# A graph transformer layer and a graph attention layer on one core: the raw weight blocks renumbered so that each load is one contiguous run, and new lists for the first and the last steps

## The chip, the core and the metric

The kernel runs on one core of a Trainium2 chip. The metric is the device time of one launch in microseconds (us). PE is TensorE, DVE is VectorE, ACT is ScalarE, POOL is GpSimd, SP is the engine that only issues transfers here.

## What is computed

There are 128 graphs of 128 nodes with 512 features, in fp32. The first layer is attention with 8 heads on a normalised input, with scores scaled by twice the adjacency; the second is graph attention with one softmax.

```python
h = jnp.maximum(_layernorm(x, axis=-1), 0.0)
q, k, v = (proj(Wq, bq), proj(Wk, bk), proj(Wv, bv))
scores = jnp.einsum('bhqd,bhkd->bhqk', q, k) * SCALE
scores = scores * (adj + adj)[:, None]
x = x + softmax(scores) @ v @ Wo.T + bo
h = jnp.maximum(_layernorm(x, axis=-1), 0.0)
Wh = h @ W
e = leaky_relu(Wh @ a[:512] + swapaxes(Wh @ a[512:], 1, 2))
x = x + elu(softmax(where(adj > 0.5, e, -9e15), axis=1) @ Wh)
```

## The kernel before, in words

**Tiling.** Two graphs make a pair (64 pairs, N = 64), two pairs make a group of four graphs. All work for a pair or group is cut into named steps, and three lists written out by hand say in which order the steps are issued. Each engine, and the transfer queue on SP, takes its own steps strictly in that order.

**Fewer products.** Q, K and V of a group are not the plain 4 x 4 x 4 block product. A fast multiplication scheme gets by with 26 block products for each of Q, K and V (TERMS), at the price of sums of blocks of the tokens (FORMS, on POOL) and of the weights (WSUMS, on DVE, made once). The weight blocks live in `w_sb`, 28 slots of three 128 x 128 blocks (Q, K and V). The sixteen raw blocks of the weights are loaded into slots 0 to 15 and many are then overwritten in place by sums.

```python
def load_blocks(n):
    nc.sync.dma_start(w_sb[:, n : C * C : C], wT[:, n : C * C : C])
def block_sum(k):
    d, a, op, b = WSUMS[k]
```

C is 4, so load n fetches slots n, n+4, n+8 and n+12: on each partition four runs of 1536 bytes. The host writes `wT` in the order of the slots.

**The lists.** HEAD (730 steps, `step@pair`) starts the kernel; ORDER (341 steps, `step:lag`) is repeated for 27 groups; TAIL (1051 steps, `step@pair`, counted back from 64) ends it. A step that has been issued is not issued again.

```python
for step, p in HEAD: do(step, p)
for g in range(EARLY, N // 2 - LATE):
    for step, lag in ORDER: do(step, 2 * g - lag)
for step, p in TAIL: do(step, N + p)
```

**Names of steps.** Several act for a later pair than the one written: with `@p`, `l0` and `t0`, `t1`, `s0` serve pair p+5, `f0`, `lT`, `hd0`, `hd1` pair p+4, and `T`, `Q`, `V`, `A`, `B` the next group.

- `lx` (L96, L98) loads a pair of x, `l0` (L103) loads x early for the statistics, `t0` and `t1` (L204 to L207, DVE) are the row statistics, `pp` (L212, POOL) the inverse root.
- `hn` (L229, DVE), `tp` (L236, PE), `ev` (L239, ACT): normalise, transpose and keep the hidden tokens `hA` of the first four pairs. Later pairs load x transposed (`lT`, L115), spread the statistics through memory (`s0`, L247; `f0`, L252) and normalise in place (`hd0` on POOL, L262; `hd1` on DVE, L264).
- `L0` to `L3` (L160) load the weight blocks, `W0` to `W34` (L166 and L169, DVE) form their sums.
- `T` (L281, POOL) forms a token sum `tf`. `Q` (L296) and `V` (L305) are the products on PE, `A` (L320 on ACT for a first take, L322 on DVE after it) and `B` (L333, L335) take them out of PSUM.
- `sc` (L373, PE), `at`, `mx`, `ex`, `rc`, `nm`: scores and softmax of a graph, `a` or `b` of the pair. `fl` (L408, DVE) turns 32 x 32 blocks, `bl` (L412, SP) sends them to memory, `pl` (L418, SP, four transfers) brings them back transposed as `aT`, `pc` (L441, PE) is the context product.
- `o0` to `o6` (L348, PE) and `od` (L455, DVE): the seven products of the output projection and their sums. `st`, `pw`, `nm`, `h2`, `d`, `px`, `pd`, `pv`, `wm`, `pr`, `m1`, `e1`, `sw`: second norm and second softmax. `g` (L534, PE), `ge` (L540, ACT), `w0` to `w6` (L348, PE), `zc` (L548, ACT), `wd` (L552, DVE): second layer.
- `lt` (L123, SP) loads the transposed adjacency. `fa` and `fb` (L564, L568, DVE) finish a pair, `so` (L574, SP) stores it; the last pair is finished in quarters (`qe`, `qa`, `qb`) and stored by `qs1`, `qs2`, `qs0` (L571, SP).

**What sets the order.** PE waits only where a step's input is not there or where none of eight PSUM banks is free. An engine that waits holds everything behind it in its own list, and SP does so too: a store that waits for its data holds the loads listed after it.

Of the kernel before, what the change touches and what calls it, by code (L numbers as in the profile page):

```python
# [13 lines left out]
P = 128  # L14
# [10 lines left out]
def kernel(  # L25
# [16 lines left out]
    nc = tc.nc  # L42
    B, S, E = x.shape
    C = E // P
# [22 lines left out]
    def sums(text):  # L67
# [7 lines left out]
        1,8,7,13- 0,10,18,10- 1,9,19,03- 0,11,0,00- 1,1,20,01+ 0,2,16,. 1,13,5,11+ 0,0,21,03- 1,12,6,12- 0,0,1,02-  # L75
        1,14,14,02- 0,18,24,00+ 0,3,26,01+ 3,20,15,03+ 2,21,22,02- 3,19,25,13+ 2,22,23,12- 3,16,9,11- 2,6,10,.
        3,17,27,01- 2,4,2,13+ 3,15,4,00- 2,4,3,10- 3,23,12,10- 2,24,8,12+ 2,7,13,11-
# [5 lines left out]
        7=15-7 16=8-4 17=15-11 18=17-16 0=1-0 19=7-18 19=19-0 9=9n11 11=9n15 5=5-11 20=5-7 6=6n5 5=14n6 21=15-3  # L83
        21=21-0 22=10n17 23=1n2 24=23-22 25=24-15 3=3+1 1=25+3 14=14n22 24=12n24 26=13-12 27=11-12 2=7+2 2=3+2 4=11-4
        3=3n19 17=8-17 12=17-12 8=19+20 8=5-8 11=5+11 13=11-13
# [55 lines left out]
    w_sb = const.tile([P, SLOTS, 3, P], F32, name="w3")  # L141
# [16 lines left out]
    def load_blocks(n):  # L158

        nc.sync.dma_start(w_sb[:, n : C * C : C], wT[:, n : C * C : C])  # L160
# [55 lines left out]
    st0, rows0, qks, vs, scs, ats, trs, blocks, aTs, pcs = ({} for _ in range(10))  # L216
# [408 lines left out]
    def listed(text, mark):  # L625
# [3 lines left out]
        lx@1 t0@-4 t1@-4 lx@0 t0@-5 pp@1 hn1@1 tp1@1 ev1@1 hn0@1 L0@0 L3@0 W2@0 W0@0 t1@-5 pp@0 W1@0 lx@2 t1@-3 tp0@1  # L629
        ev0@1 T0@-2 hn1@0 tp1@0 ev1@0 T4@-2 T8@-2 L1@0 W7@0 hn0@0 W4@0 W3@0 V0@-2 B0@-2 tp0@0 ev0@0 W8@0 W5@0 W13@0  # L630
        W9@0 Q0@-2 A0@-2 W6@0 T1@-2 Q2@-2 T2@-2 V1@-2 l0@-2 t0@-2 L2@0 t1@-2 V2@-2 T3@-2 B1@-2 V3@-2 B3@-2 B2@-2
        W14@0 Lu@0 W10@0 pp@3 hn0@3 Q1@-2 A1@-2 la@-1 W16@0 W11@0 V5@-2 V7@-2 B7@-2 Q3@-2 A2@-2 Q4@-2 V4@-2 A3@-2
        W15@0 hn1@3 W17@0 W19@0 W12@0 W18@0 W21@0 B4@-2 W20@0 W29@0 W31@0 Q5@-2 Q7@-2 A7@-2 W22@0 Lo1@0 W24@0 A4@-2
        T5@-2 Q6@-2 V6@-2 tp1@3 A6@-2 Q8@-2 Q9@-2 B6@-2 V8@-2 A8@-2 W25@0 V9@-2 Lc@0 l0@0 t1@0 T7@-2 t0@-3 t0@0 T9@-2
        T10@-2 A9@-2 Q11@-2 A11@-2 ev1@3 B9@-2 W23@0 V11@-2 tp0@3 T6@-2 Q10@-2 B8@-2 ev0@3 W26@0 W28@0 T11@-2 T12@-2
        Q13@-2 s0@0 A13@-2 A10@-2 V10@-2 Q12@-2 W27@0 W33@0 Q15@-2 A15@-2 A12@-2 B10@-2 T13@-2 V14@-2 Q14@-2 V13@-2
        B13@-2 B11@-2 A14@-2 Q17@-2 A17@-2 B14@-2 pp@2 V15@-2 V12@-2 B15@-2 T16@-2 T14@-2 Q16@-2 A16@-2 hn1@2 V16@-2
        B16@-2 Q19@-2 A19@-2 Q18@-2 Q20@-2 l0@-1 t1@-1 Q21@-2 V18@-2 V17@-2 A20@-2 hn0@2 A21@-2 W30@0 B17@-2 Q22@-2
        A22@-2 B12@-2 W32@0 T0@0 t0@-1 Q0@0 T15@-2 V20@-2 Q23@-2 A23@-2 sca@0 Lo0@0 Wo0@0 Lw0@0 scb@0 ata1@0 ata0@0
        Q24@-2 A0@0 tp0@2 ev0@2 V0@0 B20@-2 V22@-2 mxa@0 exa3@0 exa2@0 W34@0 tp1@2 l0@2 la@0 B22@-2 V24@-2 V19@-2  # L640
        ev1@2 A24@-2 Q25@-2 Lw1@0 B0@0 B24@-2 atb1@0 t1@2 t0@2 atb0@0 V25@-2 B19@-2 rca1@0 lT@0 exa1@0 exa0@0 rca0@0
        s0@-1 T1@0 T2@0 T4@0 V2@0 B2@0 Q2@0 A2@0 nma1@0 Q1@0 V1@0 Q4@0 B1@0 V21@-2 T3@0 V3@0 Wo1@0 A1@0 Q3@0 V4@0
        B25@-2 A4@0 B3@0 nma3@0 cu00@0 V5@0 A25@-2 B21@-2 mxb@0 l0@1 t0@1 t1@1 A3@0 s0@2 B4@0 nma2@0 nma0@0 fla@0
        V7@0 V23@-2 T5@0 Q6@0 A6@0 Q5@0 Q7@0 B7@0 exb1@0 A7@0 sca@1 V6@0 exb3@0 Q8@0 cu01@0 f0@0 hd0@0 V9@0 ata1@1
        exb2@0 ata0@1 rcb1@0 B6@0 V8@0 exb0@0 rcb0@0 Ww0@0 Q9@0 mxa@1 A8@0 B9@0 B8@0 lT@1 bla@0 T6@0 Q10@0 V10@0
        hd1@0 f0@1 scb@1 s0@1 nmb2@0 nmb1@0 nmb3@0 nmb0@0 flb@0 blb@0 pla@0 T7@0 T8@0 T9@0 T10@0 T11@0 T12@0 exa0@1
        atb0@1 atb1@1 V11@0 B11@0 ccp@0 V13@0 Q13@0 Wo3@0 Wo2@0 B10@0 exa3@1 A9@0 A10@0 mxb@1 A13@0 sup0@0 exb3@1
        Q11@0 A11@0 l0@4 B13@0 exa1@1 T13@0 Q14@0 V12@0 B12@0 A14@0 rca0@1 V15@0 exa2@1 B15@0 Q12@0 V14@0 plb@0
        exb0@1 Q15@0 V17@0 A12@0 Ww1@0 B14@0 exb2@1 exb1@1 rca1@1 rcb1@1 nmb3@1 nmb2@1 sua0@0 T14@0 Q16@0 hd0@1 B17@0
        V19@0 A15@0 rcb0@1 Q17@0 hd1@1 T0@2 nma2@1 nma0@1 Ww3@0 ccd@0 A16@0 t1@4 B19@0 V16@0 B16@0 A17@0 pca@0 pea@0  # L650
        nmb0@1 pcb@0 T7@2 nma1@1 o0@0 o1@0 sh@0 V21@0 B21@0 nma3@1 V18@0 Q18@0 Q20@0 sh@2 od0@0 peb@0 nmb1@1 cs0@0
        sh@1 cs2@0 cs1@0 o2@0 fla@1 bla@1 od1@0 V20@0 Q19@0 o3@0 od2@0 o4@0 flb@1 A19@0 Q21@0 A20@0 Q22@0 B23@-2
# [12 lines left out]
        T14@2 mxb@3 exb3@3 exa3@3 exb1@3 Q17@2 A17@2 T13@2 exb2@3 V14@2 B14@2 w0@0 w1@0 zc0@0 d00@1 cs0@2 d10@1
        rca0@3 o0@2 od0@2 V16@2 exb0@3 exa2@3 Q14@2 gs1@0 A14@2 cs2@2 px@1 d11@1 nma0@3 B16@2 Q19@2 o1@2 rcb0@3
        nmb1@3 w2@0 zc2@0 Q16@2 V18@2 V20@2 cs1@2 gs3@0 o2@2 w4@0 A16@2 rca1@3 cs3@2 B20@2 Ww2@0 nma1@3 l0@6 w3@0
        nma3@3 nma2@3 od2@2 rcb1@3 A19@2 fla@3 V22@2 B22@2 pd@1 pv@1 bla@3 Q18@2 Q20@2 o3@2 zc4@0 w5@0 wd4c@0 nmb3@3
        nmb0@3 nmb2@3 flb@3 od1@2 T0@4 A20@2 wm@1 Q21@2 A21@2 zc5@0 V17@2 wd1@0
# [23 lines left out]
        w6@-10 blb@-7 plb@-7 pla@-7 o4@-8 od4@-8 T16@-8 B17@-8 wd6@-10 od4c@-8 Q22@-8 A22@-8 o5@-8 pr@-9 ez@-10 m1@-9  # L693
        e1@-9 fa@-10 o6@-8 od6@-8 Q24@-8 V24@-8 V19@-8 Q0@-6 A0@-6 sw@-9 g0@-9 g1@-9 ge1@-9 ge0@-9 B19@-8 od5@-8
        B24@-8 V21@-8 T15@-8 s0@-7 f0@-6 fb@-10 st0@-8 so@-10 Q23@-8 V25@-8 A24@-8 Q25@-8 A23@-8 gs0@-9 B25@-8 st1@-8
        sca@-6 ata1@-6 ata0@-6 scb@-6 pcb@-7 peb@-7 atb0@-6 pw@-8 nm@-8 h20@-8 pca@-7 atb1@-6 h21@-8 T1@-6 Q2@-6
        w0@-9 w1@-9 B21@-8 V23@-8 pea@-7 o0@-7 mxa@-6 exa3@-6 zc0@-9 gs1@-9 gs2@-9 d00@-8 exa2@-6 exa1@-6 B23@-8
        mxb@-6 gs3@-9 A25@-8 T2@-6 V1@-6 T4@-6 T5@-6 o1@-7 w2@-9 exa0@-6 T3@-6 B1@-6 V3@-6 lT@-6 Q1@-6 lx@-7 sh@-7
        od0@-7 exb2@-6 cs0@-7 cs2@-7 od1@-7 zc2@-9 cs1@-7 rca1@-6 exb1@-6 exb0@-6 w4@-9 o2@-7 lT@-5 T8@-6 d10@-8
        rca0@-6 nma1@-6 px@-8 pd@-8 zc4@-9 A1@-6 w3@-9 pv@-8 od2@-7 cs3@-7 rcb0@-6 wd1@-9 hd0@-6 o4@-7 od4@-7 wd4c@-9  # L700
        hd1@-6 d11@-8 exb3@-6 A2@-6 V0@-6 nma0@-6 nmb0@-6 Q3@-6 o3@-7 nmb1@-6 B3@-6 d01@-8 rcb1@-6 B0@-6 o5@-7 od5@-7
        od4c@-7 w6@-9 wd6@-9 st0@-7 Q4@-6 o6@-7 V2@-6 nma2@-6 A3@-6 B2@-6 od6@-7 w5@-9 st1@-7 pw@-7 T7@-6 T9@-6
        nma3@-6 wm@-8 fla@-6 bla@-6 nm@-7 V5@-6 V7@-6 T10@-6 nmb3@-6 pr@-8 m1@-8 f0@-5 B7@-6 V4@-6 Q5@-6 Q7@-6 sca@-5
        nmb2@-6 flb@-6 blb@-6 B4@-6 A4@-6 Q6@-6 V9@-6 A7@-6 lt@-6 zc5@-9 fa@-9 Q9@-6 e1@-8 sw@-8 A6@-6 Q8@-6 ez@-9
# [235 lines left out]
```

## Time and profile before

| | us |
|---|---|
| Median of 3 runs | 2327.14 (2325.97 to 2329.51) |
| The profiled execution, its own time | 2323.18 |
| Its span, first to last instruction | 2321.4 |
| Outside the span | 1.8 |
| PE busy in the span | 2291.4 |
| DVE busy | 2099.9 |
| ACT busy | 1460.3 |
| POOL busy | 972.8 |

In this execution the steps of HEAD run until PE is at about 168.8 us, the 27 rounds of ORDER until 2084.5 us (70.95 us a round), and TAIL to the end. A busy share is an average: the head, the rounds and the tail have their own limits, so the views are read by stretches of time. The busy time of PE is a sum of modelled, overlapping ends; the distance between the starts of two matmuls tells more.

### The profile page before, as it was taken

What the parts mean: (1) busy time and instruction counts of PE and PEld (TensorE: products, weight loads), DVE (VectorE), ACT (ScalarE), POOL (GpSimd) and SP (SyncE); (2) the same over time, 40 slices, a digit from 0 to 9 for tenths busy, and PEclk for the clock granted to TensorE, in tenths of its full rate; (3) what the DMA queues carried; (4) which work ended last, traced back from release to release, by engine and by line L of the source; (5) the groups of instructions that cost most, each with busy time, mean ns of one, the idle gap of its engine ahead of it and who ended that gap; (6) DMA issues with size and microseconds to landing.
All of it is one profiled execution on the core that took longest, in us unless ns stands there. A gap on an engine that the chain in (4) does not pass through costs nothing.

```text
span 2321.4 us, 45352 instructions
## 1 busy us (share of the span) xinstructions
PE 2291.4 (99%) x15444; PEld 2037.5 (88%) x15444; DVE 2099.9 (90%) x4620; ACT 1460.3 (63%) x4942; POOL 972.8 (42%) x1112
## 2 busy tenths in 40 slices
PE   8999999999999999999999999999999999999998
PEld 6888888888888888888888888888888888888986
DVE  8998999998999999999989999999999899999897
ACT  2566666666665766666666657666666666566665
POOL 3634443443443444434434434444344344344211
PEclk9999999999999999999999999999999999999999
DMA  4544654545544545545455455454454554544432
GB/s 164 148 119 119 157 137 135 148 120 145 151 124 138 144 121 157 135 137 148 120 145 150 124 139 139 125 157 134 137 143 126 145 150 124 139 125 124 119 121 89
DMA packets 267471, 314.60 MB, mean 136 GB/s; under 512 B 23656, under 2 KB 193640, under 8 KB 267240
## 3 DMA queue, kind: packets, MB, share of 16 engines
q1 hardware_dynamic: 263736, 311.57, 48.6%
q8 instruction: 123, 2.02, 0.4%
q0 software_dynamic: 1920, 0.13, 0.1%
q14 instruction: 108, 0.88, 0.1%
q10 hardware_dynamic: 1584, 0.01, 0.0%
HBM read 210.77 MB, written 100.85 MB: 134 GB/s over the span
## 4 chain that ended last, share of the span: by engine, by line
PE 92%; DVE 4%; DMA 1%; ACT 1%; issue 1%; POOL 1%; SPq 0%; POOLq 0%; DVEq 0%; ACTq 0%
PE acc_q L296 30%; PE row_a L348 24%; PE acc_v L305 14%; PE row_c L348 9%; PE pc L441 5%; PE sc L373 5%; PE pg L534 5%; DVE st L204 1%; DVE w L169 1%; DVE qk L322 1%; ACT z L548 1%; DMA aT<-blocks 0%; DMA w<-in_wT 0%; DVE junk L478 0%; DVE x L455 0%
## 5 line engine op out<-in xcount | busy, mean ns | idle before, releaser
L296 PE MATMUL acc_q<-tf,w 128*128 128x256 f32 x2176 | 550.1, 384 | 2.2 <-DVE w L169 1.6
L281 POOL TENSOR_TENSOR tf<-hA,tf 128x256 f32<-128x256 f32 x288 | 225.0, 786 | 660.7 <-PE acc_v L305 642.4
L296 PEld LDWEIGHTS acc_q<-tf,w 128*128 128x128 f32 x2176 | 393.0, 190 | 63.0 <-ACT qk L320 8.4
L392 ACT ACTIVATE at<-at,nmx 128x128 f32<-128x128 f32 x1024 | 397.5, 391 | 35.8 <-DVE nmx L387 33.7
L322 DVE TENSOR_TENSOR qk<-qk,acc_q 128x512 f32<-128x512 f32 x512 | 341.8, 678 | 31.6 <-PE acc_q L296 28.4
L305 PEld LDWEIGHTS acc_v<-w,tf 128*128 128x128 f32 x2176 | 312.4, 191 | 24.7 <-POOL tf L281 2.1
L348 PE MATMUL row_a<-w,gT 128*128 128x256 f32 x1272 | 327.7, 384 | 4.3 <-ACT gT L540 0.7
L401 ACT ACTIVATE at<-at,rs 128x128 f32<-128x128 f32 x1024 | 329.1, 396 | 1.2 <-DVE rs L396 1.2
L305 PE MATMUL acc_v<-w,tf 128*128 128x128 f32 x2176 | 321.6, 275 | 1.9 <-POOL tf L281 1.8
L348 PE MATMUL row_a<-wo,cxT 128*128 128x256 f32 x1272 | 320.9, 382 | 0.8 <-DVE x L455 0.5
L296 PE MATMUL acc_q<-hA,w 128*128 128x256 f32 x1152 | 295.3, 380 | 0.0
L348 PEld LDWEIGHTS row_a<-w,gT 128*128 128x128 f32 x1272 | 233.6, 190 | 42.3 <-ACT z L548 8.5
L348 PEld LDWEIGHTS row_a<-wo,cxT 128*128 128x128 f32 x1272 | 231.5, 190 | 37.3 <-DVE x L455 10.0
L335 DVE TENSOR_TENSOR v<-v,acc_v 128x256 f32<-128x256 f32 x512 | 206.2, 408 | 33.1 <-PE acc_v L305 31.7
L296 PEld LDWEIGHTS acc_q<-hA,w 128*128 128x128 f32 x1152 | 208.7, 190 | 27.3 <-DVE qk L322 4.3
L380 DVE SCALAR_TENSOR_TENSOR at<-sc,adj 128x512 f32<-128x512 f32 x256 | 166.1, 681 | 44.3 <-PE sc L373 44.2
L478 DVE SCALAR_TENSOR_TENSOR junk<-h,u 128x512 f32<-128x512 f32 x256 | 200.2, 782 | 3.4 <-ACT h L471 1.0
L281 POOL TENSOR_TENSOR tf<-hA 128x256 f32<-128x256 f32 x128 | 93.4, 741 | 257.8 <-PE acc_v L305 194.0
L548 ACT COPY z<-row_a 128x256 f32<-128x256 f32 x256 | 93.3, 364 | 163.3 <-PE row_a L348 158.6
L392 ACT ACTIVATION_READ_ACCUMULATOR at<-at,nmx 128x1 f32 x1024 | 194.0, 189 | 0.0
L320 ACT ACTIVATE qk<-acc_q,bq 128x256 f32<-128x256 f32 x256 | 120.1, 469 | 113.7 <-PE acc_q L296 113.6
L269 POOL TENSOR_TENSOR x<-x,c 128x512 f32<-128x512 f32 x128 | 174.9, 1386 | 22.5 <-DMA x<-in_x 9.5
(97 smaller groups left out, 4162.8 us busy)
## 6 DMA issues: line engine op xcount, KB each, us to landing
blocks<-tr SPq DMA_DIRECT2D x128, 512.0 KB, 5.5
aT<-blocks SPq DMA_DIRECT2D x512, 128.0 KB, 3.5
x<-in_x SPq DMA_DIRECT2D x123, 512.0 KB, 4.0
out<-x SPq DMA_DIRECT2D x63, 512.0 KB, 3.3
hA<-in_xT SPq DMA_DIRECT2D x120, 256.0 KB, 4.1
mr<-rows SPq DMA_DIRECT2D x60, 256.0 KB, 3.2
adj<-in_adj SPq DMA_DIRECT2D x64, 128.0 KB, 2.2
adjT<-in_adjT SPq DMA_DIRECT2D x64, 128.0 KB, 5.5
```

The lines of the kernel that those rows point to most:

```text
L269: nc.gpsimd.tensor_tensor(xs[p][:, i, :], xs[p][:, i, :], c_sb, OP.add)
L281: eng.tensor_tensor(forms[g, 2 * C + k], form(g, a), form(g, b), OP.add if op == "+" else OP.subtract)
L296: nc.tensor.matmul(acc[:, i, :], w_sb[:, slot, i, :], form(g, f), start=fresh and i == 0, stop=True, skip_group_check=True)
L305: nc.tensor.matmul(acc[:, i, :], form(g, f)[:, i * P : (i + 1) * P], w_sb[:, slot, 2, :], start=fresh and i == 0, stop=True, skip_group_ch ...
L320: nc.scalar.activation(d[:, i, :], acc[:, i, :], AF.Identity, bias=bias[:, j : j + 1], scale=float(sign))
L322: nc.vector.tensor_tensor(d, d, acc, OP.add if sign > 0 else OP.subtract)
L335: nc.vector.tensor_tensor(d, d, acc, OP.add if sign > 0 else OP.subtract)
L348: nc.tensor.matmul(acc, left[:, la, c, :], w[:, wb, c, :], start=first, stop=c == 1, skip_group_check=True)
L380: nc.vector.scalar_tensor_tensor(ats[b][0][:, k * C : (k + 1) * C, :], scs[b][k], QSCALE, adjs[p][:, i : i + 1, :].to_broadcast([P, C, S]) ...
L392: nc.scalar.activation(at[:, j, :], at[:, j, :], AF.Exp, bias=nmx[:, j : j + 1], accum_out=sums[:, j : j + 1])
L401: nc.scalar.activation(at[:, j, :], at[:, j, :], AF.Copy, scale=rs[:, j : j + 1])
L478: nc.vector.scalar_tensor_tensor(junk, h2[:, i, :], 1.0, u_sb[:, k, :], op0=OP.mult, op1=OP.mult, accum_out=ws[:, i, 1:2] if k else src_sb ...
```

## The change

There are three parts.

1. The sixteen raw blocks get new slots: block n is in slot 4·(n mod 4) + n div 4. TERMS and WSUMS are rewritten with the new numbers and are otherwise the same list in the same order; the host writes `wT` accordingly, and a load fetches four slots side by side, one run of 6144 bytes on each partition.
2. HEAD is a new order of the same 730 steps.
3. TAIL is a new order of the same 1051 steps.

ORDER is unchanged, letter for letter. No instruction of arithmetic is added or removed.

```diff
     TERMS = list(terms("""
-        1,8,7,13- 0,10,18,10- 1,9,19,03- 0,11,0,00- 1,1,20,01+ 0,2,16,. 1,13,5,11+ 0,0,21,03- 1,12,6,12- 0,0,1,02-
+        1,8,13,13- 0,10,18,10- 1,9,19,03- 0,11,0,00- 1,1,20,01+ 0,2,16,. 1,13,5,11+ 0,0,21,03- 1,12,9,12- 0,0,4,02-
...
     WSUMS = list(sums("""
-        7=15-7 16=8-4 17=15-11 18=17-16 0=1-0 19=7-18 19=19-0 9=9n11 11=9n15 5=5-11 20=5-7 6=6n5 5=14n6 21=15-3
+        13=15-13 16=2-1 17=15-14 18=17-16 0=4-0 19=13-18 19=19-0 6=6n14 14=6n15 5=5-14 20=5-13 9=9n5 5=11n9 21=15-12
...
     def load_blocks(n):
-        nc.sync.dma_start(w_sb[:, n : C * C : C], wT[:, n : C * C : C])
+        nc.sync.dma_start(w_sb[:, n * C : (n + 1) * C], wT[:, n * C : (n + 1) * C])
...
     HEAD = """
-        lx@1 t0@-4 t1@-4 lx@0 t0@-5 pp@1 hn1@1 tp1@1 ev1@1 hn0@1 L0@0 L3@0 W2@0 W0@0 t1@-5 pp@0 W1@0 lx@2 t1@-3 tp0@1
-        ev0@1 T0@-2 hn1@0 tp1@0 ev1@0 T4@-2 T8@-2 L1@0 W7@0 hn0@0 W4@0 W3@0 V0@-2 B0@-2 tp0@0 ev0@0 W8@0 W5@0 W13@0
-        W9@0 Q0@-2 A0@-2 W6@0 T1@-2 Q2@-2 T2@-2 V1@-2 l0@-2 t0@-2 L2@0 t1@-2 V2@-2 T3@-2 B1@-2 V3@-2 B3@-2 B2@-2
-        W14@0 Lu@0 W10@0 pp@3 hn0@3 Q1@-2 A1@-2 la@-1 W16@0 W11@0 V5@-2 V7@-2 B7@-2 Q3@-2 A2@-2 Q4@-2 V4@-2 A3@-2
-        W15@0 hn1@3 W17@0 W19@0 W12@0 W18@0 W21@0 B4@-2 W20@0 W29@0 W31@0 Q5@-2 Q7@-2 A7@-2 W22@0 Lo1@0 W24@0 A4@-2
+        lx@1 t0@-4 t1@-4 L3@0 lx@0 t0@-5 pp@1 hn1@1 tp1@1 ev1@1 W2@0 hn0@1 tp0@1 W0@0 L0@0 lx@2 t1@-5 pp@0 W1@0 ev0@1
+        t1@-3 T0@-2 V0@-2 B0@-2 hn1@0 tp1@0 ev1@0 L1@0 W7@0 hn0@0 tp0@0 T4@-2 T8@-2 Q0@-2 W3@0 W4@0 W5@0 W8@0 ev0@0
+        T1@-2 T2@-2 T3@-2 A0@-2 W13@0 W6@0 Q2@-2 V1@-2 B1@-2 W9@0 V2@-2 L2@0 l0@-2 t0@-2 t1@-2 Lo0@0 Lw0@0 B2@-2 Lc@0
+        T7@-2 pp@3 T9@-2 W10@0 W14@0 W16@0 hn1@3 W11@0 A2@-2 V3@-2 B3@-2 hn0@3 W19@0 Q1@-2 A1@-2 V5@-2 V7@-2 B7@-2
+        Q3@-2 A3@-2 Q4@-2 A4@-2 V4@-2 W15@0 W29@0 W17@0 W12@0 B4@-2 Q5@-2 W25@0 W18@0 Q7@-2 A7@-2 W22@0 W20@0 T10@-2
...
-        exb2@0 ata0@1 rcb1@0 B6@0 V8@0 exb0@0 rcb0@0 Ww0@0 Q9@0 mxa@1 A8@0 B9@0 B8@0 lT@1 bla@0 T6@0 Q10@0 V10@0
-        hd1@0 f0@1 scb@1 s0@1 nmb2@0 nmb1@0 nmb3@0 nmb0@0 flb@0 blb@0 pla@0 T7@0 T8@0 T9@0 T10@0 T11@0 T12@0 exa0@1
+        s0@2 V4@0 B4@0 V21@-2 A4@0 Q3@0 T4@0 T5@0 V6@0 Ww0@0 Q6@0 T6@0 T8@0 T7@0 A3@0 Q5@0 Q7@0 nma2@0 B21@-2 V23@-2
+        rcb1@0 B6@0 V8@0 ata1@1 exb0@0 rcb0@0 nmb0@0 scb@1 A8@0 nmb2@0 mxa@1 B7@0 nmb3@0 exa2@1 lT@0 hd0@0 Q10@0
...
     TAIL = """
-        pca@-2 exa1@-1 so@-5 atb0@-1 gs1@-4 w2@-4 d11@-3 d00@-3 exa2@-1 exa3@-1 rca1@-1 pea@-2 px@-3 nma2@-1 rca0@-1
-        plb@-2 nma1@-1 atb1@-1 nma0@-1 pcb@-2 peb@-2 nma3@-1 o0@-2 gs2@-4 wd1@-4 mxb@-1 exb1@-1 exb2@-1 zc2@-4 V24@-4
-        wd1@-1 qe00@-1 gs3@-1 qa00@-1 w3@-1 qb00@-1 w4@-1 zc4@-1 wd4c@-1 w5@-1 w6@-1 qe11@-1 qa11@-1 qb11@-1 qs1@-1
-        so@-3 so@-2 zc5@-1 qa01@-1 wd6@-1 qa10@-1 qe10@-1 qb10@-1 qs2@-1 qe01@-1 qb01@-1 qs0@-1
+        exa3@-1 lt@-2 d10@-3 d11@-3 px@-3 exa1@-1 exa0@-1 rca0@-1 pla@-2 pca@-2 pea@-2 w1@-4 V24@-4 nma0@-1 rca1@-1
+        nma3@-1 plb@-2 pcb@-2 peb@-2 o0@-2 w2@-4 atb1@-1 B24@-4 gs2@-4 so@-5 mxb@-1 lx@-2 sh@-2 w3@-4 cs2@-2 V25@-4
+        zc5@-2 fa@-2 ez@-2 g0@-1 ge0@-1 g1@-1 ge1@-1 gs0@-1 gs1@-1 w0@-1 zc0@-1 gs2@-1 fb@-2 so@-2 so@-3 w1@-1 w2@-1
+        zc2@-1 wd1@-1 gs3@-1 qa00@-1 qe00@-1 qb00@-1 w3@-1 w4@-1 zc4@-1 wd4c@-1 qe11@-1 w5@-1 zc5@-1 w6@-1 qa11@-1
+        qb11@-1 qs1@-1 qe01@-1 qa01@-1 wd6@-1 qa10@-1 qe10@-1 qb10@-1 qs2@-1 qb01@-1 qs0@-1
...
-            np.transpose(np.reshape(np.stack([L0_gnn_Wq, L0_gnn_Wk, L0_gnn_Wv]), (3, 4, P, 4, P)), (4, 3, 1, 0, 2)),
+            np.transpose(np.reshape(np.stack([L0_gnn_Wq, L0_gnn_Wk, L0_gnn_Wv]), (3, 4, P, 4, P)), (4, 1, 3, 0, 2)),
```

The hunks of the lists are cut: lines of the two lists that concern the same steps stand together, and all others are left out.

## The prediction

> **What bounds the kernel now.** I read the page first for the bound.
>
> ```profile
> span 2321.4 us, 45352 instructions
> PE 2291.4 (99%) x15444; PEld 2037.5 (88%) x15444; DVE 2099.9 (90%) x4620; ACT 1460.3 (63%) x4942; POOL 972.8 (42%) x1112
> PE   8999999999999999999999999999999999999998
> PE 92%; DVE 4%; DMA 1%; ACT 1%; issue 1%; POOL 1%; SPq 0%; POOLq 0%; DVEq 0%; ACTq 0%
> ```
>
> PE is busy for 99% of the span and carries 92% of the chain that ended last; its two weak slices of forty are the first and the last. Idle time of PE is 2321.4 − 2291.4 = 30 us in all, and that is all that an order can give back, since no arithmetic changes. In the rounds of ORDER only one or two waits of about 0.2 us a round are left in the 70.95 us. So I then asked for stretches of the head and the tail.
>
> ```profile
> 0.00:11.00 11.00, 6.49 (x32) 5.82 (x32) 3.91 (x11) 2.37 (x3) 1.51 (x9) 0.97 0.82 258
> 11.00:31.00 20.00, 13.62 (x66) 11.24 (x67) 19.40 (x38) 6.99 (x17) 10.54 (x12) 0.76 0.54 205
> ...
> 60.00:80.00 20.00, 18.22 (x133) 16.37 (x133) 19.41 (x39) 18.77 (x71) 15.69 (x19) 1.00 0.44 126
> ...
> 2260.00:2280.00 20.00, 17.34 (x104) 14.00 (x100) 18.41 (x45) 15.35 (x56) 2.49 (x2) 1.00 0.53 162
> ```
>
> The columns are length, then PE, weight loads, DVE, ACT, POOL (busy us, instructions), clock, DMA share, GB/s. The reader is to see that from 11 to 31 us DVE, not PE, is full (19.40 of 20); that in 60 to 80 both are nearly full; and that PE idles most at 0 to 31. Last, who waited, and what is issued at the end:
>
> ```profile
> PE pt L236 <- DVE hn L229: 7.3, 2, 6.0
> PE pc L441 <- DMA aT<-blocks: 2.4, 2, 1.3
> PE acc_v L305 <- POOL tf L281: 1.8, 1, 1.8
> ...
> 79.67 0.71 PE L305 MATMUL acc_v<-w,tf 128*128 128x128 f32 x4 [1.78 <-POOL tf L281]
> 69.40 2.54 POOL L262 TENSOR_TENSOR hA<-hA,mr 128x512 f32<-128x512 f32 x2 [2.77 <-DMA mr<-rows]
> ...
> 2256.24 0.40 SPq L574 DMA_DIRECT2D out<-x  x1
> 2256.74 2.28 SPq L418 DMA_DIRECT2D aT<-blocks  x4
> ...
> 2314.68 0.36 SPq L571 DMA_DIRECT2D out<-x  x1
> 2315.09 0.96 SPq L574 DMA_DIRECT2D out<-x  x2
> ```
>
> **What the Trainium skill says.** "TensorE: Matmul & The Clock Gate", Part 1: PE's clock halves after an idle window of some 3.4 us. The trace agrees: PE idles from 9.28 to 15.28 us and the timeline by microseconds shows clock 0.50 from 11 to 20. "SBUF — State Buffer" says that DVE instructions with two inputs in SBUF and POOL lock each other out of a shared port pair: the weight sums (L169, L166) take 0.55 us alone and up to 1.08 beside POOL. "DMA: Bandwidth & Descriptors", Specifications: runs of 512 bytes and more reach line rate. That agrees too: with runs of 1536 bytes the loads already run at 400 GB/s (8 to 20 us).
>
> **The change, part by part.**
>
> *Contiguous loads and new numbers.* Four loads of 768 KB at 400 GB/s take 1.97 us each either way; issuing costs SP 0.54 to 1.2 us each now. SP is far ahead of DVE, so the gain lies between 0 and 0.5 us; I take 0. New slot numbers alone cost nothing: the same instructions at other addresses.
>
> *Middle.* In the issue orders of the two kernels, 4266 successive rows on PE and 3527 on DVE are the same, and the repeated list is. I take 0 for 27 × 70.95 = 1916 us; half a wait of 0.2 us in each round, either way, gives ±2.7 as bounds.
>
> *Opening, to 31 us.* L3 now goes ahead of the loads of x[0] and x[1]. By the bytes moved (0.79 MB were landed at 6.56 us, 2.62 MB at 11.19), L3 ends at 1.31 MB, about 8.0 us instead of 11.2, but x[0] at 1.57 MB, about 8.6 instead of 6.56. DVE takes t0@-5 first, so it stands idle from 6.3 to 8.6, and the first transposition on PE goes from 8.17 to about 10.2. After that DVE no longer waits for L3: its idle time ahead of 12 us is 2.3 in place of 0.2 + 2.6 = 2.8, 0.5 less. Then it is a sum of DVE steps. Up to W6, which Q2 waits for, the new list has W9 taken out (1.0 beside POOL): Q2 at 20.3 instead of 21.57. But Q6 waits for W12, and ahead of it stands one step more than before (W29, 0.47): W12 ends at 30.4 − 0.5 + 0.5 = 30.4, where it ended before, and Q6 starts at 30.6 as it did. So the gain of 1.3 at Q2 is given back at Q6: 0, with −1 and +2 as bounds (+2 if the low clock lasts for one more window of 3.4 us).
>
> *The wait at 79.67.* PE waits in V11@0 for T10. POOL had waited 2.77 us for `mr` (hd0@0) and did T6, s0@1 (3 us), T7, T8, T9 and T10 only after it. The new list has T6, T8 and T7 ahead of hd0@0 and s0@1 behind T12, so T10 is 4 to 5 us earlier, and V11@0 stands behind ccp@0, V13@0 and Q13@0, 4.8 us later. V13@0 needs T12, two POOL steps more. Gain 1.8, at least 0.5.
>
> *The wait for aT at 116.31 (1.1).* Between blb@1 and pca@1 there are now 16 PE steps rather than 9 (o2, Q20, o4, Q21, Q22, o5 more at 0.86 each and V22 at 0.44, 5.6 us). The transfer takes 5 us to land as before and so lands ahead of its use. Gain 1.1, at least 0. Moved past on SP: f0@2 and la@1, as before; nothing new is ahead of pla@1.
>
> *Other waits of the head* (0.5 at 126.7, 0.6 at 133.2): another order may keep them; 0.3 of gain taken, ±1.
>
> *Tail, 2263.29 (1.3).* Before, plb@-2 stands behind so@-5 on SP, and so@-5 waits for fb@-5 to 2256.24; then come four transfers and 4.6 us of landing. Now plb@-2 is ahead of so@-5. Its data were sent at about 2247, so it goes at about 2251.5 and lands before 2258. Gain 1.3, at least 0. What it moves past: lt@-2 is now ahead of it, but wm@-4, which frees that buffer, stands ahead of flb@-2 on DVE, so lt@-2 adds no wait. so@-5 and lx@-2 behind it are as late as before, since so@-5 still waits for fb@-5.
>
> *Other waits at 2237, 2261, 2275, 2289 (0.6, 0.5, 0.7, 0.5).* w0@-5 now has pca@-3, pcb@-3 and Q24 between V19 and itself, and w2@-4 stands behind pcb@-2 and o0@-2, so their inputs have 2 us more: 1.1 gained. The other two keep. The waits of the last 30 us (0.7 and 1.4 at 2297 and 2299) keep: g0, g1, w0, nm and w3 of pair 62 stand in the same order on PE and DVE.
>
> *The end.* so@-3 and so@-2 (1 MB, some 2.6 us at 375 GB/s) stand behind qs1 and so are issued at 2315.09, ahead of qs2 and qs0 in the queue. Now they are issued when fb@-2 is done, by about 2311, and the last 384 KB find an empty queue. The last packet ended at 2320.0; with qs0 issued at about 2317.5, 1 us until its packets and 0.7 for them, it ends at 2319.2. Gain 0.7, at most 1.5. fb@-2 (1.23 us on DVE) now stands behind gs2@-1; DVE has idle stretches of 0.6 and 1.0 there, which cover it, and if not, it costs up to 1.2 ahead of gs3 and w5.
>
> Sum: 0 + 1.8 + 1.1 + 0.3 + 1.3 + 1.1 + 0.7 = 6.3 us. Waits that a trace shows gone are in part found again at the next narrow place, since DVE has only some 8 us free from 11 to 160 us and 1.6 of 20 at 2260 to 2280; I take one fifth off: 5. Against the profiled execution, 2321.4 + 1.8 = 2323.2, that is 2318.2; the runs shown have a median 4 us above it (2327.14), so I state 2327.1 − 5 = 2322.1.
>
> **Rivals.** *The waits come back (same).* DVE is at 19.41 of 20 us in 60 to 80; if PE no longer waits for POOL there, it waits for DVE's takes, and of the head's 3.2 us only what DVE has free, 0.6 in that stretch and 0.6 in 100 to 120, is kept. With 1.3 to 2 from the tail the sum is 2.5 to 3: 2324.5. For it speaks the full DVE; against it, that in 80 to 100 DVE has 2.6 of 20 free.
>
> *The opening is late (slower).* The one place where the change moves work later is x[0] behind L3. In 2 to 6 us only 140 to 300 GB/s are moved, so x[0] may land at 11.6 rather than 8.6. All of DVE's list stands behind t0@-5, and DVE is full until 60 us: 3 us late. PE then idles for two windows, is at half clock until 24 us or later and loses 2 to 3 us in the first products. With nothing gained later: 2327.1 + 5 to 6 = 2332.5. It decides from a t0@-5 that starts after some 11 us. Against it: the rate rises to 400 GB/s from 6 us on.
>
> *The change does not do what it says.* The middle could differ in the traces though its list is the same, if the waits of one round carry over into the next; then the 27 rounds decide, by up to 2.7 us either way. It is within the range.
>
> **How the numbers follow.** A measurement of this kernel can tell about 0.2% (4.7 us) from no change. The forecast, with its own spread of 3, has 0.5 for more than 4.7 us of gain; the waits that come back, or the lower half of the forecast, 0.34; the late opening or a new wait in the tail, 0.16. The lower end is the whole sum, 6.3, with the upper bounds of the end and the middle (0.8 + 2.7) and 1 of the opening: 2316.5. The upper end takes in the first half of the late opening: 2329.5.
>
> **What would show it right or wrong.** Right: the wait of acc_v for tf near 80 us is gone; no wait of pc for aT in the tail; the stores L574 are issued ahead of the three of L571; ORDER begins on PE some 3 us earlier than 168.8, and the rounds still take 70.95. Wrong: t0@-5 starts after 11 us, the clock is at 0.5 beyond 24 us, Q6 starts after 32, a round takes another time, or new waits of PE of over 1 us stand after 31 us in the head or in the tail.

## The result, and the profile after

| | before | after |
|---|---|---|
| Median | 2326.81 us (2324.61 to 2329.70, 6 runs) | 2318.78 us (2317.52 to 2321.46, 6 runs) |
| The profiled execution, its own time | 2323.18 | 2321.46 |
| Its span | 2321.4 | 2319.6 |
| Steps of ORDER begin on PE | 168.80 | 169.01 |
| Steps of TAIL begin on PE | 2084.45 | 2086.14 |
| From there to the end | 236.95 | 233.46 |

The ratio is 0.9965, with an interval of 0.9953 to 0.9978: 8 us faster. The two profiled executions, however, are only 1.8 us apart. Before's was faster than each of its timed runs, after's is the slowest of its six. Where the other 6 us are is the question of this study.

First the page of after, with its busy times, the slices of PE and the chain.

```profile
span 2319.6 us, 45349 instructions
PE 2295.5 (99%) x15444; PEld 2042.4 (88%) x15444; DVE 2098.8 (90%) x4620; ACT 1460.9 (63%) x4942; POOL 969.7 (42%) x1112
PE   8999999999999999999999999999999999999998
PE 93%; DVE 3%; DMA 1%; ACT 1%; POOL 0%; issue 0%; SPq 0%; POOLq 0%; ACTq 0%; DVEq 0%
```

PE is still the bound. It idles for 2319.6 − 2295.5 = 24 us instead of 30, yet is busy for 4 us more with the same matmuls, so some of them ran slower. The same stretches as before:

```profile
0.00:11.00 11.00, 6.00 (x28) 5.41 (x28) 4.15 (x12) 1.28 (x1) 1.51 (x9) 0.99 0.78 256
11.00:31.00 20.00, 16.73 (x71) 13.65 (x71) 19.69 (x40) 8.17 (x19) 10.61 (x12) 0.66 0.64 235
60.00:80.00 20.00, 19.86 (x139) 17.76 (x138) 19.33 (x38) 18.50 (x73) 13.00 (x17) 1.00 0.63 172
2260.00:2280.00 20.00, 18.54 (x118) 15.62 (x118) 19.30 (x49) 16.36 (x62) 2.51 (x2) 1.00 0.49 156
```

In 60 to 80 PE is busy for 19.86 us, where it was 18.22; in the tail 18.54, where it was 17.34. From 11 to 31 the clock is 0.66, where it was 0.76. The waits of PE alone, the head from 31 to 170 us above the dots and the tail below (columns: us in total, times, longest):

```profile
PE acc_q L296 <- POOL tf L281: 2.2, 1, 2.2
PE row_a L348 <- DVE x L455: 1.2, 2, 0.8
...
PE row_c L348 <- DVE x L455: 1.5, 1, 1.5
PE row_c L348 <- DVE gT L194: 1.3, 1, 1.3
PE row_a L348 <- ACT gT L540: 0.7, 1, 0.7
```

The waits of `acc_v` for `tf` near 80 us and of `pc` for `aT` at 116 and 2263 us are gone. A new wait for `tf` has come, now of `acc_q`, which is Q10@2 at 139 us, and o6@-2 waits 1.5 us for `od4c` where it waited 0.7. The last stores on SP:

```profile
2310.61 0.91 SPq L574 DMA_DIRECT2D out<-x  x2
2313.97 2.84 SPq L571 DMA_DIRECT2D out<-x  x3
```

The two whole stores (`so`, L574) now go ahead of the three stores of the last pair's quarters (`qs`, L571).

**What took the head's gain back here.** Up to 113 us after is 3.15 us ahead: pcb@1 starts at 113.16 instead of 116.31. Then PE waits, in the timeline of PE,

```profile
139.24 1.13 PE L296 MATMUL acc_q<-tf,w 128*128 128x256 f32 x4 [2.17 <-POOL tf L281]
```

because POOL, in its own timeline, was itself held by a transfer:

```profile
135.79 2.72 POOL L262 TENSOR_TENSOR hA<-hA,mr 128x512 f32<-128x512 f32 x2 [7.01 <-DMA mr<-rows]
138.46 1.53 POOL L281 TENSOR_TENSOR tf<-hA,tf 128x256 f32<-128x256 f32 x2
```

The second row begins with T6@2, listed behind hd0@3 (L262). It is the mechanism of the old wait at 79.67, one group later. And it has a sequel, seen in windows of 2 us (last three columns: clock, DMA share, GB/s):

```profile
138.00:140.00 2.00, 0.76 (x4) 0.68 (x5) 1.05 (x3) 0.00 (x0) 1.91 (x3) 1.00 1.05 347
140.00:142.00 2.00, 2.00 (x12) 1.97 (x11) 1.02 (x2) 0.09 (x1) 1.64 (x3) 0.62 1.12 219
142.00:144.00 2.00, 2.00 (x8) 1.73 (x7) 0.42 (x1) 0.49 (x1) 0.00 (x0) 0.53 1.01 189
144.00:146.00 2.00, 2.00 (x16) 1.87 (x15) 1.73 (x5) 0.00 (x0) 1.41 (x2) 1.00 0.03 6
```

Soon after the wait PE is at half clock. The trace's record of the granted clock gives it 3.41 us, from 140.48 on, so 1.7 us more are lost. The waits of two o steps for DVE (the second row of the waits) take another 1.2. So ORDER began no earlier in this execution.

### The profile page after: what moved, and what is told of

It is laid out like the page before. It is cut to its first block, busy times and chain, and to the rows that moved or that the text cites. A ratio compares the mean times of both kernels' runs of the same rounds, so it can differ in the third digit from the quotient of the medians.

```text
span 2319.6 us, 45349 instructions
## 1 busy us (share of the span) xinstructions
PE 2295.5 (99%) x15444; PEld 2042.4 (88%) x15444; DVE 2098.8 (90%) x4620; ACT 1460.9 (63%) x4942; POOL 969.7 (42%) x1112
## 4 chain that ended last, share of the span: by engine, by line
PE 93%; DVE 3%; DMA 1%; ACT 1%; POOL 0%; issue 0%; SPq 0%; POOLq 0%; ACTq 0%; DVEq 0%
PE acc_q L296 31%; PE row_a L348 23%; PE acc_v L305 15%; PE row_c L348 9%; PE sc L373 5%; PE pc L441 5%; PE pg L534 5%; DMA w<-row 1%; ACT z L548 1%; DMA x<-in_x 1%; DVE junk L478 0%; DMA mr<-rows 0%; ACT at L401 0%; ACT at L392 0%; DVE st L204 0%
```

## The experiments

All were timed beside the kernel before, whose median was 2326.79, 2327.05, 2327.02 and 2327.59 us for the four groups below.

**1. The parts.** e1_slots has only the new slots and loads with both old lists, e2_head adds the new HEAD, e3_tail the new TAIL, e4_after both.

```diff
 e1_slots: TERMS, WSUMS, load_blocks, wT as after;  HEAD, TAIL as before
-e2_head:  HEAD as before
+e2_head:  HEAD as after
-e3_tail:  TAIL as before
+e3_tail:  TAIL as after
```

> Only the new slots and the contiguous loads, with HEAD and TAIL of the kernel before. Forecast (new slots and loads worth 0 to 0.5 us): median within 1.5 us of the kernel before, 2325 to 2328. Rival (part of the 8 us of the medians comes from the loads or the addresses): 2322 to 2324.

Measured: 2326.22, ratio 1.0001 (0.9993 to 1.0010). The slots and loads give nothing that can be seen; the interval leaves some 2 us either way. Its profiled execution has the lists of before and yet a span of 2327.0 us, 5.6 more than before's; that is taken up below.

> New slots and the new HEAD, with TAIL of the kernel before. Forecast (3.2 us of the head's waits are kept): 3 us below the kernel before, about 2323.5. Rival, read from the profiled execution of the changed kernel, where the wait at 139 us and its cold clock took back all that the head had gained: as the kernel before, 2326 to 2327. Third: the wait at 139 us cools PE only in some executions, and the median gains 3 to 5 us while the slowest execution gains nothing.

Measured: 2321.23, ratio 0.9974 (0.9963 to 0.9985): 5.6 us from the head, more than forecast. Its slowest run, 2322.52, lies below the fastest of before, 2324.03, so neither of the two rivals holds.

> New slots and the new TAIL, with HEAD of the kernel before. Forecast: the tail gains 3.1 to 3.5 us (aT wait, w0 and w2, earlier stores), about 2323.3. Rival (all 8 us of the medians come from the tail, the head keeps nothing): 2319.

Measured: 2323.20, ratio 0.9981 (0.9972 to 0.9990): 3.6 us from the tail, as forecast.

> The changed kernel once more, on the same chip as its parts. If parts add up, its gain is the sum of the gains of the new HEAD and of the new TAIL alone, less that of the slots counted twice: 6 to 8 us below the kernel before, 2318 to 2321. In its profile the wait of Q10 for the sum tf near 139 us is seen again, of 2 to 2.4 us; the theory that this wait cools PE only sometimes expects the granted clock near 140 us to differ between executions.

Measured: 2318.48, ratio 0.9961 (0.9948 to 0.9973), 8.3 us against 5.6 + 3.6 − 0.6 = 8.6: the parts add up. In this profiled execution (span 2316.6) the wait at 139 us is shorter and nothing follows it. The windows of e4_after:

```profile
136.00:138.00 2.00, 0.89 (x7) 0.64 (x5) 1.97 (x4) 0.73 (x3) 1.98 (x2) 1.00 0.82 266
138.00:140.00 2.00, 1.97 (x14) 1.87 (x14) 1.88 (x5) 0.00 (x0) 1.79 (x4) 1.00 0.99 254
140.00:142.00 2.00, 2.00 (x15) 1.87 (x14) 1.23 (x3) 0.59 (x1) 1.14 (x2) 1.00 1.13 199
```

and its POOL:

```profile
134.58 2.53 POOL L262 TENSOR_TENSOR hA<-hA,mr 128x512 f32<-128x512 f32 x2 [5.98 <-DMA mr<-rows]
```

The transfer for hd0@3 landed 1.2 us earlier, at 134.58 instead of 135.79. PE waited 1.3 us instead of 2.3 (both from the distance of two starts on PE less its usual length, as are all waits below that have no row), the clock stayed at 1.00 and ORDER began at 166.15: 2.65 us ahead of before, near the 3 predicted. Against before's profiled execution the head gives 2.65, the rounds take back 0.9 and the tail gives 3.1, in sum the 4.8 between the spans.

The old HEAD has the same sequel. In e3_tail, the wait of V11@0 for T10 near 80 us (2.4 us) ends in half clock, in before's profiled execution (1.9 us) it did not. The windows of e3_tail:

```profile
78.00:80.00 2.00, 0.00 (x0) 0.00 (x0) 1.90 (x3) 2.00 (x10) 1.92 (x2) 1.00 0.04 17
80.00:82.00 2.00, 1.94 (x9) 1.71 (x10) 2.00 (x4) 0.15 (x1) 1.47 (x3) 0.77 0.84 261
82.00:84.00 2.00, 2.00 (x7) 1.55 (x6) 0.17 (x1) 0.00 (x0) 0.00 (x0) 0.50 0.95 301
```

So a wait costs its length, and in a part of the executions another 1.7 us. What those executions have in common stands in the last section.

**2. Single edits of the changed kernel undone or mended.**

```diff
 e5_t6_first, HEAD:
-f0@3 hd0@3 B4@2 ... e1@0 sw@0 T6@2 A8@2
+f0@3 B4@2 ... e1@0 sw@0 T6@2 hd0@3 A8@2
 e6_store_ahead, TAIL:
-nma3@-1 plb@-2 pcb@-2 ... gs2@-4 so@-5 mxb@-1
+nma3@-1 so@-5 plb@-2 pcb@-2 ... gs2@-4 mxb@-1
 e7_stores_late, TAIL:
-fb@-2 so@-2 so@-3 w1@-1 ... qs1@-1 qe01@-1
+fb@-2 w1@-1 ... qs1@-1 so@-3 so@-2 qe01@-1
 e8_x0_first, HEAD:
-lx@1 t0@-4 t1@-4 L3@0 lx@0 t0@-5
+lx@1 t0@-4 t1@-4 lx@0 L3@0 t0@-5
```

> The changed kernel, with hd0@3 (POOL, waits for its transfer mr) put behind the sum T6@2. Theory: the wait of Q10@2 for T6 near 138 us was hd0@3's place on POOL, so it goes: the wait of 1.3 us (2.3 where mr lands later) is gone, and with it the cold window of 3.41 us that some executions have there. Median 1.3 to 2.5 us below the changed kernel measured on the same day (2318.5), so 2316 to 2317.2; ORDER begins on PE at about 164.9 instead of 166.15. Rival: hd1@3 on DVE and the takes behind it are now late, PE waits for DVE instead within 6 us, and the median is within 0.5 us of the changed kernel.

Measured: 2319.73, ratio 0.9969 (0.9956 to 0.9981): no gain. Q10@2 no longer waits, but POOL of e5_t6_first shows the next step behind hd0@3:

```profile
135.42 0.72 POOL L281 TENSOR_TENSOR tf<-hA,tf 128x256 f32<-128x256 f32 x1 [7.07 <-PE acc_q L296]
136.10 2.72 POOL L262 TENSOR_TENSOR hA<-hA,mr 128x512 f32<-128x512 f32 x2
138.77 0.73 POOL L281 TENSOR_TENSOR tf<-hA,tf 128x256 f32<-128x256 f32 x1
```

The last row is T11@2; T12@2 follows at 139.59, and V13@2 on PE waited 2.0 us for it until 140.36: the wait was shifted, not removed. It came back on POOL, not on DVE as the rival had it.

> The changed kernel, with the store so@-5 put back ahead of plb@-2 on SP. Theory: the store waits for fb@-5 until about 2255.8, the four transfers of plb@-2 leave after it and pcb@-2 on PE, due at 2259.8, waits until about 2262.5: a wait of pc for aT of 2.5 to 3 us is in the tail, of which a later wait (o6@-2, 1.6 us) gives up to 1 back. Median 1.5 to 3 us above the changed kernel (2320 to 2321.5). Rival (the order on SP was not what took the tail's wait away): within 0.5 us.

Measured: 2322.36, ratio 0.9979 (0.9972 to 0.9985), 3.9 us above e4_after. SP of e6_store_ahead shows the store held to 2255.20 and plb@-2 behind it:

```profile
2255.20 0.40 SPq L574 DMA_DIRECT2D out<-x  x1
2255.65 3.40 SPq L418 DMA_DIRECT2D aT<-blocks  x4
```

PE waits 2.8 us for `aT`, as the theory says, and the windows show the sequel again:

```profile
2260.00:2262.00 2.00, 0.00 (x0) 0.00 (x0) 2.00 (x7) 1.28 (x4) 0.00 (x0) 1.00 0.49 145
2262.00:2264.00 2.00, 1.96 (x17) 1.66 (x17) 0.60 (x1) 0.00 (x0) 0.25 (x1) 0.52 0.48 183
```

The expectation had only the wait, and so was 0.9 us short even at its upper end.

> The changed kernel, with the last two whole-pair stores put back behind qs1. Forecast: the end comes 0.7 us later (0.7 to 1.1, as the distance from the last w5 on PE to the end of the span went from 8.2 to 7.1 us between the two profiles): 2319.2 to 2319.6. Rival (the queue has room, the end is set by the quarter's own latency): within 0.3 us.

Measured: 2319.54, ratio 0.9968 (0.9956 to 0.9981), 1.1 us above e4_after. The medians alone do not settle a microsecond, but the time from the start of TAIL's steps to the end is 234.98 in its profile against 233.88: 1.1 us there too.

> The changed kernel, with the load of x[0] put back ahead of L3. Forecast (after 11 us the opening is a sum of DVE steps up to W12): the first transposition starts 2 us earlier, at about 8.3, and Q6 where it was, 30.5, within 0.7: no difference in the median over 0.7 us. Rival: x[0] behind L3 is what keeps PE's first idle short (it starts later but is nearer to V0), and undoing it makes the cold stretch of the opening longer by one window of 3.41 us: 1 to 2 us slower.

Measured: 2317.02, ratio 0.9958 (0.9944 to 0.9972), 1.5 us below e4_after: both theories missed. Q6 starts at 28.93 instead of 30.52. DVE of e8_x0_first:

```profile
6.65 0.69 DVE L204 BATCH_NORM_STATS2 st<-x 128x6 f32<-128x512 f32 x1 [0.37 <-DMA x<-in_x]
...
9.28 0.56 DVE L169 TENSOR_TENSOR w<-w 128x384 f32<-128x384 f32 x1 [1.08 <-DMA w<-in_wT]
```

and of e4_after:

```profile
9.17 0.69 DVE L204 BATCH_NORM_STATS2 st<-x 128x6 f32<-128x512 f32 x1 [2.79 <-DMA x<-in_x]
```

With x[0] first, DVE waits 0.37 + 1.08 us ahead of 12 us, with L3 first 2.79. As DVE is full from there to Q6, the 1.3 us come through. So this one edit of the change costs 1.6 us at Q6 in the profiles, and 1.5 in the medians, which are of five runs each and from two different groups. The execution shows one thing more: Q10@2 does not wait for T6@2 in it, since the transfer for hd0@3 landed at 131.67, 2.9 us earlier than in e4_after, though PE is only 1.6 us ahead. ORDER begins at 163.08, 3.1 us earlier than in e4_after; a stretch at half clock in the tail, 3.41 us from 2292.67, takes 1.7 back.

**3. One wait alone in the kernel before, and a version to beat both.**

```diff
 e9_before_hd0, HEAD of before:
-f0@0 hd0@0 V9@0 ... V10@0 hd1@0 f0@1 scb@1 s0@1 ... T12@0 exa0@1
+f0@0 V9@0 ... V10@0 f0@1 scb@1 ... T12@0 hd0@0 hd1@0 s0@1 exa0@1
 e10_hd0_last, HEAD of after:
-f0@3 hd0@3 B4@2 ... T11@2 T12@2 V13@2
+f0@3 B4@2 ... T11@2 T12@2 hd0@3 V13@2
 e11_best: e10's HEAD with x[0] ahead of L3, and TAIL of after:
-flb@-1 od4@-2 pr@-3 m1@-3 od4c@-2 w5@-4
+od4@-2 od4c@-2 flb@-1 pr@-3 m1@-3 w5@-4
-pw@-1 fb@-3 g1@-2 ge1@-2 g0@-2 ge0@-2 w0@-2 zc0@-2 nm@-1 h21@-1 h20@-1 gs2@-2 w3@-2 gs0@-2
+pw@-1 g1@-2 ge1@-2 g0@-2 ge0@-2 gs2@-2 fb@-3 gs0@-2 w0@-2 zc0@-2 nm@-1 h21@-1 h20@-1 w3@-2
```

> The kernel before, HEAD changed in one place: hd0@0, hd1@0 and s0@1 stand behind T12@0, so that the sums T7 to T12 no longer wait behind hd0@0's transfer on POOL. Theory (the wait at 79.67 us is worth its 1.8 us and, in a part of the executions, a cold window of 1.7 us): median 1.8 to 2.5 us below the kernel before. Rival (the waits come back): the next wait, of pc for aT at 116 us, grows by what was gained, since bl and pl hang on DVE and SP; median within 0.5 us.

Measured: 2329.33, ratio 1.0009 (1.0002 to 1.0015): slower. T10 to T12 had to wait for their buffers, hd0@0 behind them started only at 77.69, and hd1@0 held DVE. DVE of e9_before_hd0:

```profile
80.27 1.22 DVE L264 SCALAR_TENSOR_TENSOR hA<-hA,mr 128x1024 f32<-128x1024 f32 x1 [0.81 <-POOL hA L262]
```

The takes behind it on DVE, the next f0 and plb@0 were then late. pcb@0 waited 1.8 us for `aT`, and 3.41 us at half clock followed from 97.92. PE's waits from 31 to 170 us:

```profile
PE pc L441 <- DMA aT<-blocks: 2.9, 2, 1.8
PE acc_v L305 <- DVE v L335: 1.0, 2, 0.6
PE pu L605 <- DVE v L335: 0.7, 1, 0.7
```

> The changed kernel with hd0@3 put behind T12@2, not behind T6@2 only. Theory: putting hd0@3 behind T6 alone only shifted the wait to T11 and T12 (2.1 us at 140.36); behind all three, PE waits for none of them, ORDER begins 1.3 us earlier than 166.15, near 164.9, and the median is 1.3 to 2 us below the changed kernel's 2318.5. Rival: hd1@3 (DVE) or the scores of pair 3 behind it are late and PE waits there: within 0.5 us of 2318.5.

Measured: 2317.95, ratio 0.9964 (0.9951 to 0.9976), 0.5 us below e4_after, which medians do not separate. In the profile no wait for `tf` is left and ORDER begins at 165.32, 0.8 us earlier than in e4_after. A new wait of 0.4 us for a take of DVE stands at 150.45. Half theory, half rival.

> A version meant to beat both: x[0] ahead of L3 (as in e8, 2317.0), hd0@3 behind T12@2, and in TAIL od4@-2 and od4c@-2 ahead of flb@-1 (o6@-2 waits 1.6 us for od4c, which stands behind flb@-1's wait for ACT), and gs2@-2 ahead of fb@-3 and nm@-1 (w3@-2 waits 1.5 us for gs2, which stands behind nm@-1's wait for POOL). Theory: 1.2 + 1 to 1.5 us of the tail's waits go, and cold windows there become rarer: 2313.5 to 2315. Rival: DVE is full in the tail and the waits come back one step later: 2316 to 2317.

Measured: 2315.19 (2315.05 to 2316.39), ratio 0.9951 (0.9938 to 0.9965): below every run of e4_after. Its waits of PE from 2240 us on:

```profile
PE pg L534 <- ACT w L522: 1.2, 1, 1.2
PE pb L486 <- DVE junk L478: 0.8, 1, 0.8
```

o6@-2 and w3@-2 no longer wait 1.5 and 1.3 us; but g0@-3 now waits 1.2 for ACT and pb 0.8 for DVE. From the start of TAIL's steps to the end it takes 233.46 us, only 0.4 less than e4_after. For the waits of the tail the rival is right. In the head ORDER begins at 163.65, no earlier than in e8_x0_first, so with x[0] first the place of hd0@3 brought nothing more in these profiles. Of the 3.3 us below e4_after, 1.5 are those of e8_x0_first. The other 1.8 fit the theory's second part, fewer stretches at half clock: all five runs have a mean clock of 0.998, against one of five each for e8_x0_first and e4_after. That part is not shown by a run of its own.

**4. The cleaner form of the single move.** e9_before_hd0 moved hd1@0 too. So:

```diff
 e12_before_s0, HEAD of before:
-hd1@0 f0@1 scb@1 s0@1 nmb2@0 ... T12@0 exa0@1
+hd1@0 f0@1 scb@1 nmb2@0 ... T12@0 s0@1 exa0@1
```

> The kernel before with one step of HEAD moved: s0@1 (3.2 us of POOL, whose result is used only by f0@2) behind T12@0; hd0@0 and hd1@0 stay. Theory, after the move of hd0@0 and hd1@0 together had failed because hd1@0 then held DVE and the buffer of mr: T10 is 3 us earlier, the wait of V11@0 at 79.67 us goes and nothing else is late, so the median is 1.8 to 2.5 us below the kernel before (the wait, and the cold windows that it brings in some executions). Rival: the wait of pc for aT at 116 us grows by what was gained: within 0.5 us.

Measured: 2325.46, ratio 0.9994 (0.9986 to 1.0002): unclear, at most 3.3 us. V11@0 does not wait any more and ccp starts at 78.54 instead of 80.22. PE's waits from 78 to 120 us show who is next:

```profile
PE pc L441 <- DMA aT<-blocks: 1.0, 1, 1.0
PE pc L441 <- DVE at L380: 0.5, 1, 0.5
PE acc_v L305 <- DVE v L335: 0.4, 1, 0.4
```

pcb@1 starts at 116.19, before at 116.31: of the 1.7 us, 1.6 are given back within 38 us. The rival had the size right and the place wrong: the wait for `aT` is 1.0 us, where it was 1.1, and the time went to waits ahead of it, two of them for DVE. In this profile the one wait removed alone brought next to nothing; the median leaves open whether it brings more where it spares a stretch at half clock. The new HEAD keeps the gain, and it also has seven more PE steps between the sending and the use of `aT`. That these are the reason is argued from the lists; no run tests them alone.

## Why the prediction was right

The direction, the chance given most weight and the range held, with 2318.78 inside 2316.5 to 2329.5. That the range held is in part luck. A gain of 8 us is more than the whole sum of 6.3; the lower end, which by its own terms is 2316.3, went beyond that sum chiefly by 2.7 us for the middle and 1 for the opening, and neither came. By its own steps:

- **Contiguous loads 0:** right (e1_slots). An issue on SP took 0.54 to 0.67 us before, though, and not up to 1.2.
- **Opening 0:** right in sum. Q2 at 20.45 (20.3 predicted), Q6 at 30.62 (30.6), first transposition at 10.38 (10.2), t0@-5 at 8.78. The rival of the late opening is real in kind: e8_x0_first shows that L3 ahead of x[0] costs 1.5 us; it stayed small because x[0] came well before 11 us.
- **Wait at 79.67, 1.8:** 2.1 (ccp at 78.06 instead of 80.22). **Wait at 116.31, 1.1:** 1.0 more, 3.15 in all by pcb@1.
- **Other head waits 0.3, and the sign "ORDER begins on PE some 3 us earlier":** 2.65 in e4_after, −0.2 in after's profiled execution. The step that failed here is that it counted no new wait in the head. T6@2 stands behind hd0@3 in the new list, as T6@0 stood behind hd0@0 in the old; in the five profiles with this HEAD that takes 0.9 to 2.3 us, and in one of them the clock too.
- **Tail, 1.3 + 1.1 + 0.7 = 3.1:** right, 3.5 and 3.1 in the two profiles, 3.6 in the medians; e6_store_ahead and e7_stores_late show the parts. Wrong in one: "the other two keep", as o6@-2 waits 1.6 us, where it waited 0.9.
- **Middle 0:** nearly. In before all rounds take 70.95. In every kernel with a new HEAD three of 27 take at least 71.08 (V11 takes 0.1 us longer in them); ORDER is the same letter for letter, and why this happens was not found. Single rounds of up to 71.7 come on top in some executions, but not through the new HEAD alone: e1_slots, with the old one, has two of 71.96 and 71.72. Both together cost 0.9 in e4_after.
- **One fifth off, for waits that come back:** right in size, 5.0 against the 4.8 between the spans of before and e4_after. The loss came chiefly as the wait at 139 us (1.3 in e4_after) and as the longer rounds (0.9).
- **The median by adding 4 us to the profiled execution:** the term that was mis-sized. The prediction took the 4 us between before's profile and its median as a fixed offset that the change keeps. In e4_after the profiled execution is the median.
- **Its signs of being wrong:** three came. Rounds took another time, new waits of over 1 us stand in the head (2.2) and in the tail (1.5), and in after the opening is at half clock until 24.43 us. None of them undid the gain.

The offset is where the 8 us come from. 4.8 us are seen between before's profile and e4_after's. The other profiles show that before's was a fortunate execution. With the old HEAD the steps of ORDER begin on PE at 168.80, 170.86 and 170.94 us (before, e1_slots, e3_tail), with the HEAD of after at 165.59 to 169.01, median 166.15 of five. From the start of TAIL's steps to the end the old TAIL takes 236.3 to 239.2 us, median 237.6 of five profiles, and the TAIL of after 233.4 to 235.5, median 234.2 of six. These differences, 4.7 and 3.4 us, less 0.9 in the rounds, make 7.2 of the 8.3 between before and e4_after.

The timed runs point the same way. Over the 90 runs of before made beside the twelve experiments, the mean granted clock is 0.9956, and the time goes with it: 13 runs at 0.994 have a mean of 2329.5 us, 24 at 0.995 2327.7, 42 at 0.996 2326.4 and 10 at 0.997 2325.5, about 1.4 us for 0.001. Of 11 runs of the changed kernel 9 are at 0.997 and one at 0.998; their mean is 0.9970. So 0.0014 × 1.4 / 0.001 = 2 us of the 8 go with the clock. This is a rough estimate of half-clock time that no longer occurs, since slow runs may have longer waits too, and the mean also counts the half clock of the opening and of the last microseconds. The parts fit it: all seven runs of e2_head are at 0.997, where the thirteen of e1_slots are at 0.994 to 0.997. The waits themselves also differ from execution to execution: the wait for T10 was 1.9 us in before's profile but 2.5 and 2.4 in e1_slots and e3_tail, the wait for `aT` in the tail 1.45 there but 1.86, 1.62, 1.59 and 2.00 in four others with the old TAIL. How the 8 us divide between length and clock rests on few profiles; it is argued, not shown.

The rival of the waits that come back is also true, for single edits: the profiles of e5_t6_first, e9_before_hd0 and e12_before_s0 show it.

## What to carry to other kernels

Where PE is the bound, count a wait as its length plus its chance of a stretch at half clock, count short waits within some 3.4 us as one, and look at the spread of the timed runs and their clocks, not at one profile, to see what waits cost. Removing one wait can be worth little until the next narrow place has slack as well: follow the list for another 40 us and count the steps between a transfer's issue and its use. A step that waits for a transfer belongs behind all steps on its engine that PE needs earlier, and not only behind the first of them, provided that what needs the step itself can wait so long: in e10_hd0_last it could, in e9_before_hd0, where hd1@0 on DVE needed it, it could not.

## What the runs showed of the hardware

The half clock after a wait comes in units: the trace's record has stretches of 3.413, 6.827, 10.240 and 13.653 us. In each of the fourteen profiles the changes of the clock inside the span lie whole numbers of 3.413 us apart, on a grid whose place differs from execution to execution. "TensorE: Matmul & The Clock Gate", Part 1, of the Trainium skill says that PE goes cold after an idle window of some 3.4 us. Here waits well below that were followed by 3.41 us at half clock: 2.3 us in after, 2.4 in e3_tail, 2.95 in e6_store_ahead; 1.3 us in e4_after, 1.9 in before and 2.5 in e1_slots were not. The measurement decides: short waits can cool PE, in some executions and not in others.

The grid tells these executions apart. For each of its intervals between 31 and 2312 us, 9340 in all profiles, PE's idle time was added up, from modelled ends to the next starts. The ten intervals that half clock follows have 1.74 to 2.79 us. Of the others only two have so much, 1.77 in e5_t6_first and 1.90 in e1_slots, where the boundary at 79.20 cuts the wait of 2.5 us, and the rest have 1.73 or less. So the wait of e3_tail near 80 us, whole inside one interval (77.68 to 81.10, 2.21 us idle), cooled PE, and that of before, cut at 78.62 into 0.73 and 1.05, did not. Two waits close together, w0@-2 (0.84 us) and w3@-2 (1.5 us, some 2.5 us later), cooled PE in five of the thirteen profiles that have both: there they put 1.74 to 2.02 us into one interval, in the other eight at most 1.73. In these runs, then, half clock follows idle time of about half an interval, and the place of the grid is the chance in it. This was read from the profiles afterwards; no run was made to test it, and the two exceptions stay open.

The longer cold stretch of the opening, 13.65 us in after and 10.24 in e4_after, cost nothing with the new HEAD: Q6 started at 30.62 and 30.52, since DVE sets the pace there. With the old HEAD it may cost: Q6 started at 31.40 in e1_slots (13.65 us cold) and at 30.67 in before (10.24).

A contiguous load is cheaper to issue: 0.33 us on SP in e1_slots at the median against 0.59 with four runs per partition in before. It moved nothing, since SP was ahead.
